# Reordering one attention step on TensorE: the next step's first product earlier, the second products in four pieces

## The chip, the cores and the metric

The kernel runs on one core of one Trainium2 chip. The metric is the device time of that core in microseconds (us), the median of several executions. The engines are named as the profile names them: PE is TensorE's matmuls and PEld its weight loads, DVE is VectorE, ACT is ScalarE, POOL is GpSimd, and SP is the engine whose queue issues most DMAs.

## What is computed

The program has two graph layers over 3327 nodes with 128 features. Layer 0 is an aggregation over the adjacency matrix, two small products, a batch normalisation and a residual. Nearly all of the time goes to layer 1, an attention over all nodes that is carried out 128 times with 8 channels each. Cut to what matters:

```
q = (x @ Wq.T).reshape(d, n, h)          # d = 128, n = 3327, h = 8
k = (x @ Wk.T).reshape(d, n, h)
v = (x @ Wv.T).reshape(d, n, h)
a = einsum('dnh,dmh->dnm', q, k) * scale
a = softmax(a + adj + adj, axis=2)
out = einsum('dnm,dmh->dnh', a, v).reshape(n, h * d)
return x + out @ Wo.T
```

The softmax needs no separate pass for its sum: `v` carries a ninth column of ones, so that the second product gives the sum of the exponentials beside the weighted values.

## The kernel before

**Tiling.** The 128 attentions are taken in 32 groups of `G` = 4 (index `i`). The nodes `n` of the result are cut into seven blocks (index `y`): six of 512 columns and one of 255. The nodes `m` are cut into `NC` = 26 chunks of 128. For one group and block there are 26 chunks times 4 attentions, and these are handled as 52 *pairs*: a pair is one chunk `c` and one `half`, that is two of the four attentions. A step (index `s`, 13 for each block) takes four pairs. There are 32 x 7 x 13 = 2912 steps, all written out in one list `steps`.

**Two ways for a pair.** In a step the first three pairs are `plain` and the fourth, `rest`, is weighted. (The last step of a block has two plain pairs and two weighted ones.) A plain pair goes from PSUM through DVE, which adds the adjacency (`add`, line 818), and the three of a step then go together through one exponential on ACT (`late`, line 856). A weighted pair goes straight from PSUM through an exponential on ACT (line 828) and is then multiplied on POOL by weights that were made once (line 831). The exponential of a step's plain pairs is issued one step later, behind the first weighted exponential of that step, hence its name `late`.

**First product.** `product(i, y, c, half)` (line 725) makes the scores of one pair: two matmuls of 32 rows by 128 columns of weights, at rows 64*half and 64*half+32, each over 512 columns, into one PSUM tile `s` of two banks. There are three such tiles, which go round: a product waits until the tile of the product three places earlier was read. The four products of a step will be called w (weighted), p0, p1 and p2 (plain).

**Second product.** `weigh` (line 604) multiplies the exponentials of one pair and one attention by `v`: 128 rows by 9 columns, at columns 32*b of the array, where b = 2*half + x is the attention, adding into one PSUM bank `av` for each block. The second products of a step are done `LAG` = 3 steps later. They are eight `weigh` calls, two for each of the four pairs, called S0, S1, S2 and S3 here. In the halves of a step's pairs 0 and 1 alternate (0, 1, 0, 1 or 1, 0, 1, 0), except in the last step of a block, where they are 0, 1, 1, 0.

**Order.** The order on every engine is that of the Python calls; no planner moves anything. One step of the kernel before is, on PE:

```
w  p0 | S0 S1 | p1 p2 | S2 S3 |
```

Between S1 and p1 stands `step()`, which once for each block issues, one step apart, a copy of `av` on DVE, four transposes on PE (line 619), a division on DVE and a DMA. Between p2 and S2 stands `beside()`, which from time to time issues a projection for later groups (line 196) or a part of the output of an earlier one (lines 257 and 265). `fetch` issues the DMAs of the adjacency and the weights two steps ahead, and `loads` those of the next group's `q`, `k` and `v`.

Of the kernel before, what the change touches and what calls it, by code (L numbers as in the profile page):

```python
# [30 lines left out]
SU = NC // 2  # L31
# [13 lines left out]
def tile_two_layer_gnn(  # L45
# [73 lines left out]
    def tile_set(x):  # L119
        q = qkp.tile([P, NP], F32R, name=f"q{x}")  # L120
        k = qkp.tile([P, NC, P], F32R, name=f"k{x}")
        v = qkp.tile([P, G, NC, H + 1], F32, name=f"v{x}")

        nc.vector.memset(v[96:, :, NC - 1, :], 0.0)
        return q, k, v

    sets = [tile_set(x) for x in range(2)]
# [109 lines left out]
    def projections(wk, hj, j, quick, ov, factor):  # L237
        return [
            projection(wk, hj, j, s, e, quick, ov, factor) for s in (1, 0, 2) for e in range(2)
        ]  # L240
# [36 lines left out]
    def drive(part, bank=None):  # L277

        if bank is not None:
            next(part)  # L280
            part.send(bank)
        else:
            next(part, None)


    with tc.tile_pool(name="l0", bufs=1) as l0, tc.tile_pool(
# [125 lines left out]
        for c in range(NC):  # L412
# [16 lines left out]
            i = c - 2 * NQ - 5  # L429
# [59 lines left out]
        for i, (n0, w) in enumerate(blocks):  # L489
            s = slice(n0, n0 + w)  # L490
# [112 lines left out]
    def weigh(tiles, av, w, e, b, c, first, last):  # L603
        nc.tensor.matmul(  # L604
            av[32 * b : 32 * b + H + 1, :w], tiles[2][:, b, c, :], e,
            start=first, stop=last,
        )
# [44 lines left out]
    def attention():  # L652


        with tc.tile_pool(name="adj", bufs=4) as ap, tc.tile_pool(
# [17 lines left out]
            if True:  # L673
                steps = [
                    (i, y, s)
                    for i in range(NG) for y in range(len(blocks)) for s in range(SU)
                ]

                def at(i):
                    return i * G  # L680

                def pairs(s):


                    last = s == SU - 1
                    plain = [(j // 2, j % 2) for j in range(3 * s, 3 * s + 3 - last)]
                    rest = [(WC + s // 2, 1 - s % 2)]
                    return plain, rest + ([(NC - 1, 0)] if last else [])
# [3 lines left out]
                for x, (i, y, s) in enumerate(steps):  # L692
                    n0, w = blocks[y]
# [4 lines left out]
                    c = pairs(s)[1][0][0]  # L698
# [19 lines left out]
                def product(i, y, c, half):  # L718
                    q, k, _ = sets[i % 2]
                    n0, w = blocks[y]  # L720
                    we = w + w % 2
                    p = psc.tile([P, 2, NB], F32, name="s")
                    for x in range(2):
                        rs = slice(64 * half + 32 * x, 64 * half + 32 * x + 32)
                        nc.tensor.matmul(  # L725
                            p[:, x, :we], k[rs, c, :], q[rs, n0 : n0 + we],
                            start=True, stop=True,
                        )
                    return p
# [26 lines left out]
                def beside(i, y, s):  # L756


                    for j in [1, 2] if i == 0 else [i + 2] if i + 2 < NG else []:
                        if (y, s) != (0 if i else 3 * (j - 1), 3):  # L760
                            continue
                        hj = wk.tile([P, CH], F32, name="hj")
                        nc.sync.dma_start(hj, hd[:, j * CH : (j + 1) * CH])
                        extra.extend(projections(wk, hj, j, False, ov, low_half[:CH, 1:2]))
                    if s in (8, 11) and extra:
                        drive(extra[0])
                    if s in (9, 12) and extra:
                        drive(extra.pop(0))
                    if s in (7, 10) and extra:
                        drive(extra[0], avs2[(i * len(blocks) + y + 1) % 2])  # L770
                    if (y, s) == (2, 12) and i:
                        extra.extend(outputs(wk, i - 1))

                extra = []

                def second(part):

                    (i, y, s), es = waiting[0]
                    n0, w = blocks[y]
                    av = avs2[(i * len(blocks) + y) % 2]  # L780
                    ps = sum(pairs(s), [])
                    for j in (0, 1) if part == 0 else (2, 3):
                        c, half = ps[j]
                        for x in range(2):
                            weigh(
                                sets[i % 2], av, w, es[j][:, x, :w], 2 * half + x, c,
                                s == 0 and part == 0, s == SU - 1 and part == 1,
                            )
                    if part:
                        waiting.pop(0)  # L790
                        if s == SU - 1:
                            ending.append(finish(rp, av, at(i), n0, w))

                def step():
                    for g in ending[:1]:
                        if next(g, g) is g:
                            ending.pop(0)

                for x, (i, y, s) in enumerate(steps):
                    n0, w = blocks[y]  # L800
                    fetch(x + PRE)
                    k = x - i * SU * len(blocks) - FROM[i]
                    if k == 0 and i + 1 < NG:
                        pending = loads(sets[(i + 1) % 2], at(i + 1))
                        total = len(pending)

                    while pending and (total - len(pending)) * (SU * len(blocks) - FROM[i] - 4) <= k * total:
                        pending.pop(0)()
                    more_weights(i, y, s)
                    due = len(waiting) == LAG  # L810
                    plain, rest = pairs(s)
                    d = ep.tile([P, 3, 2, NB], F32, name="d")
                    es = [d[:, j] for j in range(len(plain))]

                    def add(j, p):
                        c = plain[j][0]

                        nc.vector.scalar_tensor_tensor(  # L818
                            d[:, j, :, :w],
                            have[0, i, y, c // 2][:, c % 2, :w]  # L820
                            .unsqueeze(1).to_broadcast([P, 2, w]),
                            SAFE / 2, p[:, :, :w], ALU.min, ALU.add,
                        )

                    def weighted(c, half):
                        f = fp.tile([P, 2, NB], F32, name="f")
                        p = product(i, y, c, half)
                        nc.scalar.activation(  # L828
                            f[:, :, :w], p[:, :, :w], AF.Exp, scale=2.0
                        )  # L830
                        nc.gpsimd.tensor_tensor(  # L831
                            f[:, :, :w], f[:, :, :w],
                            have[1, i, y, c][:, :w].unsqueeze(1).to_broadcast([P, 2, w]),
                            ALU.mult,
                        )
                        es.append(f)

                    weighted(*rest[0])
                    if late is not None:
                        late()  # L840
                    add(0, product(i, y, *plain[0]))
                    if due:
                        second(0)
                    step()
                    add(1, product(i, y, *plain[1]))
                    if len(rest) > 1:
                        weighted(*rest[1])
                    else:
                        add(2, product(i, y, *plain[2]))
                    beside(i, y, s)  # L850
                    if due:
                        second(1)

                    def late(d=d, w=w, n=len(plain)):
                        flat = d[:, :n].rearrange("p j x n -> p (j x) n")[:, :, :w]
                        nc.scalar.activation(flat, flat, AF.Exp, scale=2.0)  # L856

                    waiting.append(((i, y, s), es))
                late()
                while waiting:  # L860
                    second(0)
                    step()
                    second(1)
                while ending:
                    step()
                for p, b in zip(outputs(wk, NG - 1), (0, 1, 0)):
# [75 lines left out]
    def general():  # L942
# [65 lines left out]
        with tc.tile_pool(name="gw2", bufs=2) as wk, tc.tile_pool(  # L1008
# [3 lines left out]
            for j in range(NG):  # L1012
                for p, b in zip(outputs(wk, j), banks):
                    drive(p, b)
                    drive(p)
                    drive(p)

    attention()
    needed = nc.values_load(flag[0:1, 0:1], min_val=0, max_val=1)
    with tc.If(needed > 0):  # L1020
# [43 lines left out]
```

## Time and profile before

| what | value |
|---|---|
| median of 3 runs | 10516.94 us (10514.26 to 10520.51) |
| the profiled execution's own time | 10527.91 us |
| span of its instructions | 10526.1 us |
| mean granted TensorE clock | 0.986 |
| DVE line 818, adjacency of one plain pair | 8512 instructions, mean 1138 ns |
| ACT line 856, exponential of the plain pairs | 2912, mean 2532 ns |
| ACT line 828, exponential of a weighted pair | 3136, mean 970 ns |
| POOL line 831, weights on a weighted pair | 3136, mean 2235 ns |
| PE line 725, first products | 23296 records, mean 482 ns |
| PE line 604, second products | 34048 + 12544 records, mean 569 and 571 ns |

The mean of an instruction counts from its start to its end. On ACT and DVE the next one often starts a little before the end of the one ahead, and on PE several run at once, so counts times means exceed the busy time. The distance from start to start is what an engine really spends. The profile has two records for each FP32 `weigh` call (34048 + 12544 = 46592 = 16 for each of 2912 steps, where the code has eight calls), so eight calls are sixteen records; the first products have one record for each matmul.

### The profile page before, as it was taken

The page shows a single profiled execution, that of the slowest core. Times are in us where ns is not written, and L with a number is a line of the kernel's source. Part 1 is how long each engine was busy: PE and PEld are TensorE (multiplying, and loading weights), DVE is VectorE, ACT ScalarE, POOL GpSimd, SP SyncE. Part 2 cuts the span into 40 slices and gives each one's busy share as a digit, 9 for nine tenths or more (in the row PEclk, how much of TensorE's full clock was granted, in tenths as well). Part 3 has the DMA queues.
Part 4 walks back from the last instruction along what each step waited for, and adds up shares of the span by engine and source line. Part 5 has one row for each costly group of instructions (what it writes and reads, how often), then busy time and mean ns, then how long its engine had stood idle before and what let it go on. Part 6 is the DMA issues. An engine that isn't in the chain of part 4 may idle for free. (4 is left out here: it accounts for less than half of the span.)

```text
span 10526.1 us, 186778 instructions
## 1 busy us (share of the span) xinstructions
PE 9922.7 (94%) x72399; PEld 2813.8 (27%) x72399; DVE 9714.9 (92%) x9949; ACT 9948.5 (95%) x6200; POOL 7497.1 (71%) x3868
## 2 busy tenths in 40 slices
PE   7889999999999999999999999999999999999999
PEld 3222222222222222222222222222222222222222
DVE  5789999999999999999999999999999999999998
ACT  4889999999999999999999999999999999999998
POOL 0667777777777777777777777777777777777776
PEclk8899999999999999999999999999999999999999
DMA  7655555555555555555555555555555555555554
GB/s 241 192 168 163 157 168 165 163 162 160 162 166 165 164 162 157 161 170 163 160 162 157 165 170 165 160 158 163 164 169 163 162 163 158 165 165 167 156 152 128
DMA packets 1115761, 1731.67 MB, mean 165 GB/s; under 512 B 198350, under 2 KB 441932, under 8 KB 1107180
## 3 DMA queue, kind: packets, MB, share of 16 engines
q1 hardware_dynamic: 1110478, 1713.99, 56.3%
q8 instruction: 568, 9.31, 0.4%
q10 hardware_dynamic: 4350, 5.64, 0.2%
q14 instruction: 333, 2.73, 0.1%
q0 software_dynamic: 32, 0.00, 0.0%
HBM read 1618.76 MB, written 100.53 MB: 163 GB/s over the span
## 5 line engine op out<-in xcount | busy, mean ns | idle before, releaser
L818 DVE SCALAR_TENSOR_TENSOR d<-at,s 128x1024 f32<-128x1024 f32 x8512 | 9204.3, 1138 | 642.7 <-PE s L725 406.2
L831 POOL TENSOR_TENSOR f<-f,wt 128x1024 f32<-128x1024 f32 (+1 forms) x3136 | 6983.8, 2235 | 2619.1 <-ACT f L828 2572.0
L856 ACT ACTIVATE d<-d 128x3072 f32<-128x3072 f32 (+1 forms) x2912 | 7372.9, 2532 | 73.4 <-DVE d L818 70.5
L604 PE MATMUL av<-d,v 128*9 128x512 f32 x34048 | 5528.5, 569 | 0.1
L725 PE MATMUL s<-q,k 32*128 32x512 f32 x23296 | 4280.7, 482 | 505.7 <-DVE d L818 218.0
L725 PEld LDWEIGHTS s<-q,k 32*128 32x128 f32 x23296 | 1773.9, 182 | 5829.2 <-DVE d L818 3312.2
L828 ACT ACTIVATE f<-s 128x1024 f32<-128x1024 f32 (+1 forms) x3136 | 3014.8, 970 | 313.8 <-PE s L725 252.3
L604 PE MATMUL av<-f,v 128*9 128x512 f32 x12544 | 2864.0, 571 | 0.0
L604 PEld LDWEIGHTS av<-d,v 128*9 128x9 f32 x34048 | 630.7, 88 | 1381.6 <-issue 1265.4
L604 PEld LDWEIGHTS av<-f,v 128*9 128x9 f32 x12544 | 310.6, 88 | 52.9 <-issue 41.0
L180 POOL CAST k<-ks 128x256 fp32r<-128x256 f32 x434 | 284.2, 655 | 0.0
L416 PE MATMUL acc<-a,A 128*128 128x512 f32 (+1 forms) x364 | 151.3, 568 | 24.0 <-ACT A L350 23.3
L619 PEld LDWEIGHTS av<-ident,avs 128*128 128x128 f32 (+1 forms) x864 | 121.1, 208 | 179.9 <-issue 178.8
L226 POOL TENSOR_TENSOR o<-pf,o 104x512 fp32r<-104x512 f32 x124 | 160.4, 1293 | 9.9
L619 PE MATMUL av<-ident,avs 128*128 128x128 f32 (+1 forms) x864 | 163.8, 311 | 0.6 <-DVE avs L612 0.6
L225 POOL CAST o<-pf 104x512 fp32r<-104x512 f32 x124 | 75.8, 611 | 115.3 <-DVE pf L224 59.8
L612 DVE COPY avs<-av 128x512 f32<-128x512 f32 (+1 forms) x224 | 144.2, 644 | 2.8 <-PE av L604 2.8
L423 DVE TENSOR_REDUCE amax<-a 128x1 f32<-128x3327 f32 x26 | 93.7, 3610 | 37.7 <-DMA a<-in_adj 37.7
L416 PEld LDWEIGHTS acc<-a,A 128*128 128x128 f32 x364 | 68.8, 192 | 108.8 <-issue 84.4
L420 ACT ACTIVATE junk<-a 128x3327 bf16<-128x3327 f32 x26 | 77.4, 2977 | 6.6 <-DMA a<-in_adj 6.5
L389 POOL TENSOR_TENSOR sq<-wk 128x512 f32<-128x512 f32 x2 | 2.1, 1040 | 102.3 <-PE aside L390 102.3
L629 DVE TENSOR_TENSOR oq<-av,ri 128x128 f32<-128x128 f32 (+1 forms) x224 | 64.1, 286 | 7.7
(120 smaller groups left out, 952.0 us busy)
## 6 DMA issues: line engine op xcount, KB each, us to landing
at<-in_adjT SPq DMA_DIRECT2D x1728, 512.0 KB
wt<-wd SPq DMA_DIRECT2D x1344, 256.0 KB
at<-in_adjT SPq DMA_DIRECT2D x288, 255.0 KB
ks<-kT SPq DMA_DIRECT2D x496, 104.0 KB
q<-qT SPq DMA_DIRECT2D x496, 104.0 KB
at<-in_adjT SPq DMA_DIRECT2D x192, 256.0 KB
a<-in_adj SPq DMA_DIRECT2D x26, 1663.5 KB
wt<-wd SPq DMA_DIRECT2D x224, 127.5 KB
```

Of the source, the lines that this page charges most:

```text
L180: nc.gpsimd.tensor_copy(k[:, c : c + n, half * 64 : half * 64 + 64], ks.bitcast(F32).rearrange("g (p c) -> g c p", c=NC)[:, c : c + n, :],)
L226: nc.gpsimd.tensor_tensor(o[:CH, 1], f[:CH], o[:CH, 0].bitcast(F32), ALU.subtract)
L416: nc.tensor.matmul(acc[i][:, :w], A[:, c, :], a[:, n0 : n0 + w], start=(c == 0), stop=(c == NC - 1),)
L423: nc.vector.tensor_reduce(amax[:, c : c + 1], a[:, :N], AX.X, ALU.max, apply_absolute_value=True)
L604: nc.tensor.matmul(av[32 * b : 32 * b + H + 1, :w], tiles[2][:, b, c, :], e, start=first, stop=last,)
L612: nc.vector.tensor_copy(avs[:, :w], av[:, :w])
L619: nc.tensor.transpose(pt[:R, j, :], avs[:, j : j + (R - 1) * J + 1 : J], ident)
L725: nc.tensor.matmul(p[:, x, :we], k[rs, c, :], q[rs, n0 : n0 + we], start=True, stop=True,)
L818: nc.vector.scalar_tensor_tensor(d[:, j, :, :w], have[0, i, y, c // 2][:, c % 2, :w] .unsqueeze(1).to_broadcast([P, 2, w]), SAFE / 2, p[:, ...
L828: nc.scalar.activation(f[:, :, :w], p[:, :, :w], AF.Exp, scale=2.0)
L831: nc.gpsimd.tensor_tensor(f[:, :, :w], f[:, :, :w], have[1, i, y, c][:, :w].unsqueeze(1).to_broadcast([P, 2, w]), ALU.mult,)
L856: nc.scalar.activation(flat, flat, AF.Exp, scale=2.0)
```

## The change

The change alters only the order in which PE's instructions are issued. `second` no longer takes a half (two pairs) but one pair, and is called four times in a step: ahead of p0, between p0 and p1 (twice, with `step()` between the two), and between p1 and p2. The w of the next step is issued by `first(x + 1)`, right behind the last product of this step and ahead of `beside`, and its tile is carried over in `coming`. One step on PE is then:

```
S0 | p0 | S1 S2 | p1 | S3 | p2 w(next) |
```

```
-                def second(part):
+                def second(j):
+                    if not due:
+                        return
...
-                    for j in (0, 1) if part == 0 else (2, 3):
-                        c, half = ps[j]
-                        for x in range(2):
-                            weigh(
-                                sets[i % 2], av, w, es[j][:, x, :w], 2 * half + x, c,
-                                s == 0 and part == 0, s == SU - 1 and part == 1,
-                            )
-                    if part:
+                    c, half = ps[j]
+                    for x in range(2):
+                        weigh(
+                            sets[i % 2], av, w, es[j][:, x, :w], 2 * half + x, c,
+                            s == 0 and j < 2, s == SU - 1 and j >= 2,
+                        )
+                    if j == 3:
                         waiting.pop(0)
...
+                def first(x):
+                    i, y, s = steps[x]
+                    return product(i, y, *pairs(s)[1][0])
+
+                coming = first(0)
                 for x, (i, y, s) in enumerate(steps):
...
-                    weighted(*rest[0])
+                    weighted(rest[0][0], coming)
                     if late is not None:
                         late()
+                    second(0)
                     add(0, product(i, y, *plain[0]))
-                    if due:
-                        second(0)
+                    second(1)
                     step()
+                    second(2)
                     add(1, product(i, y, *plain[1]))
+                    second(3)
                     if len(rest) > 1:
-                        weighted(*rest[1])
+                        weighted(rest[1][0], product(i, y, *rest[1]))
                     else:
                         add(2, product(i, y, *plain[2]))
+                    if x + 1 < len(steps):
+                        coming = first(x + 1)
                     beside(i, y, s)
-                    if due:
-                        second(1)
```

The number of instructions on each engine is the same as before. The order on DVE, ACT, POOL and SP is the same too.

More of the change, by code (lines that the diff above doesn't have):

```diff
@@ L823, in add, with weighted @@
                         )
-                    def weighted(c, half):
+                    def weighted(c, p):
                         f = fp.tile([P, 2, NB], F32, name="f")
-                        p = product(i, y, c, half)
                         nc.scalar.activation(
@@ L859, in attention @@
                 late()
+                due = True
                 while waiting:
-                    second(0)
+                    for j in range(4):
+                        second(j)
                     step()
-                    second(1)
                 while ending:
```

## The prediction

> **What bounds the kernel now.** I read the page's busy shares first, then who ACT waits for, and then the timeline of one step.
>
> ```profile
> PE 9922.7 (94%) x72399; PEld 2813.8 (27%) x72399; DVE 9714.9 (92%) x9949; ACT 9948.5 (95%) x6200; POOL 7497.1 (71%) x3868
> ```
>
> Three engines look equally full, so busy shares settle nothing. ACT's timeline does:
>
> ```profile
> 5004.17 2.82 ACT L856 ACTIVATE d<-d 128x3072 f32<-128x3072 f32 x1
> 5006.83 1.07 ACT L828 ACTIVATE f<-s 128x1024 f32<-128x1024 f32 x1
> 5007.73 2.83 ACT L856 ACTIVATE d<-d 128x3072 f32<-128x3072 f32 x1
> ```
>
> From 5004.17 to 5007.73 is one step, 3.56 us, with no idle time: ACT sets the pace. DVE is close behind: three additions that ran from 5005.28 in 3.48 us. ACT's waits (us in total, times, longest):
>
> ```profile
> ACT f L828 <- PE s L725: 252.3, 380, 7.6
> ACT d L856 <- DVE d L818: 70.5, 212, 0.6
> ```
>
> So 252 us is all that an earlier w could give back. Now PE in the same stretch, in order of start:
>
> ```profile
> 5004.75 0.51 PE L725 MATMUL s<-q,k 32*128 32x512 f32 x4
> 5005.18 0.60 PE L604 MATMUL av<-d,v 128*9 128x512 f32 x2
> 5005.20 0.60 PE L604 MATMUL av<-f,v 128*9 128x512 f32 x2
> 5005.62 0.60 PE L604 MATMUL av<-d,v 128*9 128x512 f32 x2
> 5005.63 0.60 PE L604 MATMUL av<-f,v 128*9 128x512 f32 x2
> 5006.16 0.90 PE L725 MATMUL s<-q,k 32*128 32x512 f32 x4
> 5006.99 1.04 PE L604 MATMUL av<-d,v 128*9 128x512 f32 x8
> 5007.97 0.50 PE L725 MATMUL s<-q,k 32*128 32x512 f32 x4
> 5008.40 0.60 PE L604 MATMUL av<-d,v 128*9 128x512 f32 x2
> ```
>
> Read the starts, not the durations. Two second-product pairs (four column groups, eight records) run as two rounds: four records at 5005.18, four at 5005.62, 0.44 us apart. The next first product starts 0.54 us after the second round; the whole run costs 5006.16 - 5005.18 = 0.98 us, and so does the next (5007.97 - 5006.99). Two first products together cost 5005.18 - 5004.75 = 0.43 us. A first product alone:
>
> ```profile
> 5010.65 0.50 PE L725 MATMUL s<-q,k 32*128 32x512 f32 x2 [0.77 <-DVE d L818]
> 5011.08 1.05 PE L604 MATMUL av<-d,v 128*9 128x512 f32 x8
> ```
>
> costs the same 0.43 us. So PE now needs 2 x 0.98 + 2 x 0.43 = 2.82 us of a step's 3.56; its 94% is mostly how the records' ends are counted. In the block of 255 columns:
>
> ```profile
> 5107.86 0.62 PE L604 MATMUL av<-d,v 128*9 128x255 f32 x8
> 5108.41 0.39 PE L725 MATMUL s<-q,k 32*128 32x256 f32 x4
> 5108.73 0.39 PE L604 MATMUL av<-d,v 128*9 128x255 f32 x2
> ```
>
> the two prices are 0.55 and 0.32 us.
>
> **What the Trainium skill says.** "TensorEngine Tiling (Array Packing)", Key Properties, says "Mode switching requires drain". First products use row tiles and second products column tiles, so each bar in the step's order is such a switch. The trace agrees: 0.54 us where the rounds are 0.44 apart. "TensorE: Matmul & The Clock Gate", Part 3, The mechanism, says tiles overlap when they don't share a row group; here different halves share none (two products in 0.43 us). Its section Back-to-back issue gap gives N/2.4 ns + 2.5 ns, 216 ns for 512 columns, where they cannot overlap. The trace bears this out roughly: the first products' median record is 496 ns, that of 256 columns 376, or 120 ns for 256 columns. "Perfetto Trace Analysis", Identifying the Most-Contended Engine, warns that matmul busy share is no measure of headroom; the 2.82 us above is the case in point.
>
> **The change, part by part.** No instruction is added or removed. DVE, ACT, POOL and SP keep their order, so their durations stay and no DMA is moved past another; the edits in `weighted` and the closing loop cost nothing. What changes is PE's runs: a step has three runs of second products and three of first products in place of two and two.
>
> *Second products in quarters.* S0 and S3 are each one pair: two column groups, two records each. The two records of one group are the ones that start 0.44 us apart, so half a run still takes two rounds and the drain: 0.98 us, not 0.49. The trace of before has no lone pair; the bounds are 0.49 (half the work) and 0.98 (same rounds). I take 0.98, since the rounds are seen and only their width shrinks. A step's three runs cost 2.94 us.
>
> *First products.* p0 alone 0.43, p1 alone 0.43, p2 with the next w 0.43 plus what their collision costs. The halves of plain pairs alternate and go on with the next step's w, so p2 and the next w have the same half: same rows, so no overlap. Bounds: 0 and a second 0.43; I take 0.22 by the page's price and the 120 ns. Together 1.51 us.
>
> A 512-column step then needs 2.94 + 1.51 = 4.45 us of PE against ACT's 3.56. **PE becomes the bound.**
>
> *Do waits add to that?* Put S0 at 0: p0 at 0.98, S1 S2 at 1.41, p1 at 2.39, S3 at 2.82, p2 at 3.80, w at 4.02, next S0 at 4.45. With a first product ready 0.49 us after its start and additions of 1.16, DVE ends p0's at 2.63, p1's at 4.04, p2's at 5.45, that is 1.00 into the next step. p1 needs the PSUM tile that p2's addition freed at 1.00, 1.39 before its turn; the next w needs p0's addition, 1.39 before its turn; p2 needs the weighted exponential (0.06 to 1.1), 2.7 before. Behind a waiting w would stand S0 and p0, but none waits. ACT starts the late exponential at 1.00, ends at 3.8, and then idles until w comes. The second products' data are three steps old. So the queue runs without waits, at PE's price.
>
> *The sum*, in us. 512 columns: 192 blocks, 2496 steps.
> - Second products: 3 x 2496 runs, and 192 more because `step()` puts the transposes between S1 and S2 once a block: 7680 x 0.977 (5006.158 less 5005.181 in the record) = 7503. In a block's last step S1 and S2 have the same half, two rounds more: 192 x 0.87 = 167.
> - First products: 3 x 2496 x 0.43 = 3220; collisions in 12 steps of 13, 2304 x 0.22 = 507.
> - Transposes: 192 x 0.68 = 131.
>
> 255 columns: 32 blocks, 416 steps: 1280 x 0.55 + 32 x 0.43 + 1248 x 0.32 + 384 x 0.11 + transposes 17 = 1176. Beside it, by their start-to-start times: 186 projections x 1.036, 62 output turns x 0.51 and 31 output products x 1.92 = 284. In all 11528 + 1176 + 284 = 12988 us, where before took 10198 (second products run from 308.1 to 10506). Ahead of it stay 308 us, behind it 20. Span 13316, own time 1.8 more, 13318. The runs' median lies 11 us below the profiled 10527.9, so about **13,300 us**, 26% slower.
>
> **Rivals.**
> 1. *A quarter costs half a run* (0.49). Then PE needs 0.49 + 0.98 + 0.49 + 1.51 = 3.47 us, under ACT's 3.56; w is ready early and the 252 us go, less the 20 or so of the start-up: about 10,285 us, **faster**. It decides below (3.56 - 0.98 - 1.51)/2 = 0.535 us for a lone pair. For it: half the columns, half the products. Against it: the two rounds are of one column group, each already 0.44 us, so 0.87 even without a drain.
> 2. *The switch is hidden*, and only passes count: three runs of 0.87 and four products of 0.22, 3.49 us, again just under ACT: no gain that PE's lack of slack leaves, about 10,520. Against it: at every switch in the timeline the drain is there, both ways (0.54 for 0.44, 0.43 for 0.22).
> 3. *Heavier than forecast*: p2 and w cost a full 0.86 us together (+0.21 x 2304 + 0.1 x 384 = 522), so 13,830; with the clock of 0.986 in place of 1, some 1% more, 13,950.
> 4. *The order doesn't change*: excluded, the built order shows the three runs.
>
> **How the numbers follow.** What I forecast, with rival 3 as its upper side, has 0.95; rival 1 0.03; rival 2 0.02. A measurement here tells about 0.2% (21 us) from no change. The low end is a collision that costs nothing (-507 - 42, 12,750) with 50 off for lone pairs that drain sooner, 12,700; the high end is 13,950. Rivals 1 and 2 lie outside.
>
> **What would show it.** In the profile after: PE's timeline with S0 and S3 as runs of two by two records, 0.98 us to the next start; ACT's idle time before line 828, released by PE line 725, risen from 252 to some 2,000 us or more; DVE's idle time behind PE alike; `issue`, not DVE or ACT, ahead of the weight loads of line 725. Lone pairs at 0.5 us, or ACT back to back, would prove it wrong; p2 to S0 in 0.43 or 0.86 would prove the collision's size wrong.

## The result and the profile after

The changed kernel takes 13278.62 us (13273.48 to 13282.60) against 10517.81 us before, a ratio of 1.2625 with a 95% interval of 1.2603 to 1.2647. That is 2761 us slower. The forecast was 13,300. The profiled execution's span is 13279.4 us at a mean granted clock of 0.995. Before it was 0.986, so a lower clock is not what made it slower.

The page's busy shares, which before stood at 92 to 95% on three engines, now come apart:

```profile
PE 13137.5 (99%) x72399; PEld 3286.3 (25%) x72399; DVE 10191.5 (77%) x9949; ACT 10425.7 (79%) x6200; POOL 7481.7 (56%) x3868
```

The chain that ended last, by engine and by line, now reaches back through nearly the whole execution and stays on PE:

```profile
PE 97%; DVE 2%; ACT 1%; DMA 1%; issue 0%; POOL 0%; ACTq 0%; DVEq 0%; POOLq 0%; SPq 0%
PE av L604 61%; PE s L725 31%; DVE d L825 1%; PE av L196 1%; PE av L619 1%; PE acc L416 1%; PE av L265 0%; ACT f L834 0%; PE av L257 0%; DMA q<-qT 0%; DMA xs<-in_x 0%; ACT A L350 0%; ACT junk L420 0%; PE aside L406 0%; DMA a<-in_adj 0%
```

ACT's waits (us in total, times, longest) show the other side of it. Line 828 of before is now line 834, and 856 is 864:

```profile
ACT f L834 <- PE s L725: 2500.6, 2709, 7.6
ACT d L864 <- DVE d L825: 65.5, 262, 0.6
```

The wait for the first products was 252.3 us before; the wait for the additions is where it was. The two together grew by 2243 us, and ACT's busy time by 477 (10425.7 - 9948.5), because instructions that used to start before the one ahead had ended now start apart (their mean durations hardly changed: 2532 to 2521 ns and 970 to 963). The sum of the two, 2720 us, accounts for the longer span (2753 us) but for some 30.

What ended the idle time of PE's weight loads has changed as well:

```profile
PEld s L725 <- issue: 5320.4, 6722, 1.7
PEld av L604 <- issue: 2226.0, 7563, 0.8
PEld s L725 <- DVE d L825: 902.5, 1101, 6.4
```

Before, 3312.2 us of that idle time ended with an addition on DVE and 826.0 with "issue". Now 5320 of 7022 us end with "issue", that is, with nothing that the profile shows but PE's own turn; additions still end 902.5. The matmuls of line 725 themselves waited for other engines for 40 us in all, where they had waited for 390 before:

```profile
PE s L725 <- ACT f L834: 25.2, 65, 11.4
PE s L725 <- DVE d L825: 15.0, 19, 5.9
```

One step of PE's timeline:

```profile
5007.00 0.50 PE L725 MATMUL s<-q,k 32*128 32x512 f32 x2
5007.43 1.03 PE L604 MATMUL av<-f,v 128*9 128x512 f32 x4
5008.39 0.73 PE L725 MATMUL s<-q,k 32*128 32x512 f32 x4
5009.05 1.03 PE L604 MATMUL av<-d,v 128*9 128x512 f32 x4
5010.01 0.50 PE L725 MATMUL s<-q,k 32*128 32x512 f32 x2
5010.44 1.05 PE L604 MATMUL av<-d,v 128*9 128x512 f32 x8
5011.42 0.50 PE L725 MATMUL s<-q,k 32*128 32x512 f32 x2
```

Read the starts. S3, one pair alone (four records), costs 5008.39 - 5007.43 = 0.96 us, and so does S0 (5010.01 - 5009.05). Two pairs together, eight records, cost 5011.42 - 5010.44 = 0.98. Half the work takes nearly the same time. p2 and the next w take 5009.05 - 5008.39 = 0.66 us, where two first products of different halves took 0.43 before.

### The profile page after: what moved, and what is told of

The parts are those of the page before. It is cut to its first block, busy times and chain, and to the rows that moved or that the text cites. A ratio compares the mean times of both kernels' runs of the same rounds, so it can differ in the third digit from the quotient of the medians.

```text
span 13279.4 us, 186778 instructions
## 1 busy us (share of the span) xinstructions
PE 13137.5 (99%) x72399; PEld 3286.3 (25%) x72399; DVE 10191.5 (77%) x9949; ACT 10425.7 (79%) x6200; POOL 7481.7 (56%) x3868
## 4 chain that ended last, share of the span: by engine, by line
PE 97%; DVE 2%; ACT 1%; DMA 1%; issue 0%; POOL 0%; ACTq 0%; DVEq 0%; POOLq 0%; SPq 0%
PE av L604 61%; PE s L725 31%; DVE d L825 1%; PE av L196 1%; PE av L619 1%; PE acc L416 1%; PE av L265 0%; ACT f L834 0%; PE av L257 0%; DMA q<-qT 0%; DMA xs<-in_x 0%; ACT A L350 0%; ACT junk L420 0%; PE aside L406 0%; DMA a<-in_adj 0%
## 5 line engine op out<-in xcount | busy, mean ns | idle before, releaser
L825 DVE SCALAR_TENSOR_TENSOR d<-at,s 128x1024 f32<-128x1024 f32 x8512 | 9677.4, 1144 | 2919.0 <-PE s L725 2601.5
L864 ACT ACTIVATE d<-d 128x3072 f32<-128x3072 f32 (+1 forms) x2912 | 7340.6, 2521 | 98.7 <-DVE d L825 65.5
L604 PE MATMUL av<-d,v 128*9 128x512 f32 x34048 | 5909.8, 564 | 0.0
L834 ACT ACTIVATE f<-s 128x1024 f32<-128x1024 f32 (+1 forms) x3136 | 2997.0, 963 | 2562.1 <-PE s L725 2500.6
L725 PE MATMUL s<-q,k 32*128 32x512 f32 x23296 | 4815.2, 455 | 43.6 <-ACT f L834 25.2
L725 PEld LDWEIGHTS s<-q,k 32*128 32x128 f32 x23296 | 1918.0, 182 | 7022.1 <-issue 5320.4
L604 PE MATMUL av<-f,v 128*9 128x512 f32 x12544 | 3045.6, 564 | 0.0
L604 PEld LDWEIGHTS av<-d,v 128*9 128x9 f32 x34048 | 670.9, 88 | 1691.8 <-issue 1544.4
L604 PEld LDWEIGHTS av<-f,v 128*9 128x9 f32 x12544 | 351.5, 88 | 798.6 <-issue 681.6
L612 DVE COPY avs<-av 128x512 f32<-128x512 f32 (+1 forms) x224 | 144.7, 646 | 2.9 <-PE av L604 2.9
L196 PE MATMUL av<-wk,hj 128*104 128x512 f32 x124 | 68.5, 635 | 0.0
```

The source lines that it names most:

```text
L196: nc.tensor.matmul(bank[:CH], hj, wqk[s][:, e * NB : (e + 1) * NB], start=True, stop=True)
L604: nc.tensor.matmul(av[32 * b : 32 * b + H + 1, :w], tiles[2][:, b, c, :], e, start=first, stop=last,)
L612: nc.vector.tensor_copy(avs[:, :w], av[:, :w])
L725: nc.tensor.matmul(p[:, x, :we], k[rs, c, :], q[rs, n0 : n0 + we], start=True, stop=True,)
L825: nc.vector.scalar_tensor_tensor(d[:, j, :, :w], have[0, i, y, c // 2][:, c % 2, :w] .unsqueeze(1).to_broadcast([P, 2, w]), SAFE / 2, p[:, ...
L834: nc.scalar.activation(f[:, :, :w], p[:, :, :w], AF.Exp, scale=2.0)
```

## The experiments

Four runs ask what the 2761 us are made of, and four more whether the early w is worth something by itself. "Before" ran beside each of them, at 10514.67 to 10516.05 us.

### e1: the early w alone

```
+ add(0, product(i, y, *plain[0]))
  second(0); second(1)
  step()
  add(1, product(i, y, *plain[1]))
  ... p2, coming = first(x + 1), beside ...
+ second(2); second(3)
```

> Only one part of the change: the next step's w stands behind p2, but the second products keep two runs a step (p0 | S0 S1 | p1 p2 w | S2 S3). The theory of PE prices (a run of second products 0.97 us whatever its width, a lone run of first products 0.43, p2 with w 0.66) gives 2 x 0.98 + 0.43 + 0.66 = 3.05 us of PE in a 512-column step, under ACT's 3.56, so ACT sets the pace again: 10,300 to 10,520 us, ACT's wait for the first products below the 252 us of before. The rival theory, that the early w does the harm because it holds one of three PSUM tiles for longer, gives 13,000 us or more here.

Measured: 10791.53 us, ratio 1.0262 (1.0248 to 1.0276). The rival's 13,000 is out, so the early w is not what made the changed kernel 26% slower. But my own range was wrong too: it is 2.6% slower than before. ACT's waits:

```profile
ACT d L864 <- DVE d L825: 350.9, 838, 1.1
ACT f L834 <- PE s L725: 97.3, 100, 7.2
ACT f L834 <- PE av L604: 83.1, 166, 4.6
```

The wait that the early w aims at, ACT's wait for the first products, did fall, from 252 to 97 us. In its place the wait for additions rose from 70.5 to 350.9, and a new one of 83 us came up: the weighted exponential waits for second products on PE. By the program that is a tile `f` which is free only after S3, and S3 now stands behind w. The three waits grew by 208 us in all and ACT's busy time by 62 (10010.9 against 9948.5), 270 of the 272 us of longer span. PE's own waits and one step of the timeline show where the additions are held up:

```profile
PE s L725 <- DVE d L825: 591.5, 1307, 5.5
```

```profile
5005.47 1.19 PE L725 MATMUL s<-q,k 32*128 32x512 f32 x6
...
5006.15 0.18 PEld L725 LDWEIGHTS s<-q,k 32*128 32x128 f32 x2 [0.46 <-DVE d L825]
...
5006.59 0.10 PEld L604 LDWEIGHTS av<-d,v 128*9 128x9 f32 x3 [0.25 <-issue]
```

The run p1 p2 w begins at 5005.47. The weight loads of its third product, w, stand still until an addition on DVE ends, and only at 5006.59 can S2 begin: 1.12 us for a run that costs 0.66 without a wait. This step is no exception: over the 512-column steps the median of such a run is 1.03 us. S2, S3 and the next p0 stand behind w in PE's queue and are late with it, and so is the addition on p0.

### e2: the three runs alone, w where it was

```
- weighted(rest[0][0], coming)
+ weighted(rest[0][0], first(x))
  add(0, ...); second(0); second(1); step()
  add(1, ...); second(2)
  ... p2; beside; second(3) ...
```

> The other part alone: three runs of second products a step, w where it was before (w p0 | S0 S1 | p1 | S2 | p2 | S3). PE prices give 0.976 + 2 x 0.963 + 3 x 0.43 = 4.19 us in a 512-column step and 2.56 in a 255-column one: 10,463 + 131 + 1,066 + 17 + 284 + 328 = about 12,290 us. The rival (the early w does the harm) gives about 10,520, the time of before.

Measured: 12493.52 us, ratio 1.1881 (1.1859 to 1.1903). The rival's 10,520 is out; the three runs alone make most of the loss. The sum was 203 us too small. In the trace 171 us of that are runs S0 S1 that took longer than their price before the next first product, some 90 us in blocks of 512 columns and 80 in the block of 255. They are waits of that product, p1, which the sum had left out. PE's waits name what ended them:

```profile
PE s L725 <- ACT f L833: 131.0, 562, 10.8
PE s L725 <- DVE d L824: 18.8, 33, 6.4
```

Where p1 waits, it mostly starts 0.05 us after the end of the same step's weighted exponential, while the last addition had ended 0.88 us before (medians of 610 such waits). In other steps p1 does not need that exponential: in one at 5004.84 us it starts 0.21 us before its end. Three tiles that strictly go round would make p1 wait for the addition on p2; why it waits for w in some steps stays open.

### e3: the other half for the weighted pair

```
- rest = [(WC + s // 2, 1 - s % 2)]
- return plain, rest + ([(NC - 1, 0)] if last else [])
+ rest = [(WC + s // 2, s % 2)]
+ return plain, rest + ([(NC - 1, 1)] if last else [])
```

> The changed kernel with the halves of the weighted pairs exchanged, so that p2 and the next w lie in different row groups, and S1 and S2 of a block's last step in different column groups. Nothing else changes. If the collision of p2 and w is what lifts 0.43 to 0.66, it goes: 2304 x 0.23 + 384 x 0.12 = 576 us, and 192 x 0.85 + 32 x 0.42 = 176 us for the last steps: about 12,530 us. If that step is long for another reason (a wait inside the run), about 13,280 stays.

Measured: 12562.80 us, ratio 1.1947 (1.1925 to 1.1969), 716 us less than the changed kernel where 752 were expected. In PE's timeline p2 and w are now one run of the short kind, 5003.13 - 5002.70 = 0.43 us:

```profile
5002.70 0.50 PE L725 MATMUL s<-q,k 32*128 32x512 f32 x4
5003.13 1.03 PE L604 MATMUL av<-d,v 128*9 128x512 f32 x4
5004.10 0.50 PE L725 MATMUL s<-q,k 32*128 32x512 f32 x2
```

The instructions and their order are the same; only the row groups differ, and in a block's last step the column groups of S1 and S2. So the 0.23 us of p2 and w are the price of two products on the same rows, which do not run side by side, and not a wait inside the run.

### e4: every pair alone

```
  second(1); step()
+ add(1, product(i, y, *plain[1]))
  second(2)
  ... p2 ...
+ second(3)
  coming = first(x + 1)
```

> One more switch there and back in each step: every pair alone (S0 | p0 | S1 | p1 | S2 | p2 | S3 | w). If the cost is the number of runs, 4 x 0.963 + 4 x 0.43 = 5.57 us in a 512-column step and 4 x 0.535 + 4 x 0.313 = 3.39 in a 255-column one: 13,908 + 131 + 1,411 + 17 + 284 + 328 = about 16,080 us. If the cost were the work of the second products spread over narrower runs, with little for the switch, it would stay near 13,300.

Measured: 16081.07 us, ratio 1.5293 (1.5265 to 1.5321). The sum was 16,080. PE's timeline is the plainest of all:

```profile
5004.04 1.03 PE L604 MATMUL av<-d,v 128*9 128x512 f32 x4
5005.01 0.50 PE L725 MATMUL s<-q,k 32*128 32x512 f32 x2
5005.43 1.03 PE L604 MATMUL av<-d,v 128*9 128x512 f32 x4
```

A pair alone costs 0.97 us and a first product alone 0.42, with two of the four column groups or row groups unused each time. The second products are the same in number as before, in the same 16 records a step; what grew is the number of runs. In these kernels the cost is by the run.

### e6 and e7: can the early w be had without the wait?

```
  add(0, ...); second(0); second(1); step()
  add(1, ...); second(2); second(3)
  ... p2; coming = first(x + 1); beside ...
e7: the same, with beside(i, y, s) right behind add(0, ...)
```

> Early w and two full runs of second products, but cut elsewhere: S0 S1 between p0 and p1, S2 S3 between p1 and p2, so that p2, the next w and the next p0 stand together (p0 | S0 S1 | p1 | S2 S3 | p2 w). PE price 2 x 0.98 + 0.43 + 0.66 = 3.05 us, the same as in e1. The theory on e1 is that w waits inside its run for the addition on p0, issued only 1.4 us earlier, with S2 S3 and the next p0 queued behind it, so that the additions run late (ACT's wait for them 373 us in place of 71). Here 2.8 us lie between p0 and w, so that wait goes: ACT's wait for line 825 near 70 us, its wait for the first products at or below 100, S3 ahead of w so that no tile f is waited for: 10,300 to 10,450 us. If an early w harms by itself, about 10,790 as in e1.

> As e6, with the projections and output products (beside) moved from between w and the next p0 to behind that p0, ahead of S0 S1. If e6 still loses time where such a product (up to 1.92 us) delays p0 and with it DVE, this is faster than e6 by up to 32 x 9 x 0.5 = some 50 to 150 us; if the additions are fed anyway, the same within 0.3%.

Measured: e6 10893.02 us, ratio 1.0365 (1.0350 to 1.0380); e7 10886.45 us, ratio 1.0358 (1.0344 to 1.0372). Both are slower than e1, and where `beside` stands makes no difference in this order. e7's saving of 50 to 150 us did not come; its other branch, the same within 0.3%, did. The expectation for e6 was wrong. ACT's waits in e6:

```profile
ACT f L834 <- PE s L725: 437.2, 612, 7.5
ACT d L864 <- DVE d L825: 144.7, 386, 0.7
```

The additions are less late than in e1 (144.7 for 350.9; the 373 in the expectation counts the shortest gaps too, which this list leaves out) and no tile `f` is waited for, as expected. But w itself is now later than before the change, 437 against 252 us. PE still waits for additions at line 725:

```profile
PE s L725 <- DVE d L825: 487.5, 789, 5.8
```

The run of three has a median of 1.02 us, where its price is 0.66. Its last product is p0 now, which by the round of three tiles needs the tile that p1's addition frees. The expectation had looked only at w.

The loss is not in every step. From one exponential of line 864 to the next, the undisturbed steps of a 512-column block take as long as before (the 2nd step of a block: 3.56 us before and in e1, 3.57 in e6). The means over each block's 13 steps, summed, go from 47.9 us before to 48.7 (e1) and 49.1 (e6) in a 512-column block, and from 30.1 to 32.4 and 33.5 in the block of 255 columns (groups 3 to 31). Over all groups the 192 wide blocks lose 205 us in e1 and 256 in e6, and the 32 narrow ones 70 and 110. That is all of the 272 and 365 us by which the spans grew. For each step the narrow block loses the most; in a wide block most of the excess stands in single steps. One place is where a projection falls: the 7th to 9th step take 11.19 us together before, 11.53 in e1 and 11.59 in e6. By its prices PE has spare time in all of these orders (3.05 of 3.56 us). That they lack room to catch up after a disturbance is a reading of these figures and not shown by a run of its own, and which of the waits matters in the narrow block was not tried.

### e8 and e9: aimed at the disturbed steps

```
e8, from e1:  coming = first(x + 1) if s in (7, 10) else None
              weighted(rest[0][0], coming or first(x))
e9, from before:  beside(i, y, s) moved to right behind add(0, ...)
```

> The kernel before, with w ahead only in the two steps a block (the 8th and the 11th) in which a projection or output product follows p2: p1 p2 w | projection | S2 S3 | p0. In the trace of before the steps at these places take 4.07 and 3.85 us from one exponential of line 856 to the next, in place of 3.56: 0.51 + 0.29 = 0.80 us a block, 192 blocks, about 150 us in all that a late w can cost there. If w's lateness is what is lost, 10,370 to 10,480 us. If, as in e1 and e6, the late p0 then holds DVE up and the loss only changes its name, about 10,520 or up to 100 more.

> The kernel before, its order of runs untouched, with the projections and output products moved from between p2 and S2 to behind the next p0, ahead of S0. w and p0 are then no longer late by up to 1.9 us; p1 is. If feeding ACT and the first addition in time is what counts, some 50 to 150 us less than before: 10,370 to 10,470. If p1 is as urgent, since its addition follows 1.2 us after p0's, 10,500 or more.

Measured: e8 10630.57 us, ratio 1.0111 (1.0095 to 1.0126); e9 10565.41 us, ratio 1.0048 (1.0034 to 1.0062). Neither beats before: both are slower, by less than 2% but outside their intervals. ACT's waits in e8, then in e9:

```profile
ACT f L834 <- PE s L725: 294.4, 514, 7.4
ACT d L863 <- DVE d L825: 116.5, 332, 0.7
```

```profile
ACT f L828 <- PE s L725: 227.0, 349, 8.4
ACT d L856 <- DVE d L818: 142.5, 448, 0.6
```

In e9 the wait for first products fell by 25 us and the wait for additions rose by 72: the loss changes its name, as its second expectation had it, and the difference of 47 us is about the 45 by which the span grew. In e8 even the wait for first products rose. It was a mistake to read 252 us as a sum to be won by serving w first. The likely reason is that w, p0 and p1 come due within about one addition of each other (1.14 us), so that in one queue what serves one of them delays the next.

## Why the prediction was right, step by step

- **PE becomes the bound: right.** The chain stays on PE for 97%, and its weight loads wait mostly on "issue". e4 carried the same sum one run further, with prices read again from the trace of after, and met it within about 1 us in 16,081.
- **A quarter costs as much as a half: right, and 1.4% too dear.** A lone run took 0.963 us (median from start to start between 1000 and 10,000 us of the trace), where I had used 0.977; for 5376 lone runs (two a step, and two more in each of 192 blocks, where the transposes part S1 from S2) that is 75 us too much. The trace of before had no lone pair to read this price from, and rival 1 stood on it, with 0.49.
- **First products: right.** p0 and p1 alone took 0.430 us each.
- **The collision of p2 and w: right, a little small.** 0.662 us against the 0.65 taken: 28 us over 2304 steps. e3 shows the cause to be the common rows. The Trainium skill's section "Back-to-back issue gap" in "TensorE: Matmul & The Clock Gate", which the prediction used for this size, gives its 216 ns as the gap of a single isolated matmul and a smaller figure for a stream of them. That it holds where two cannot overlap was the prediction's own reading; the 0.232 us measured here are near it.
- **The last step of a block: right.** S1 and S2 on the same columns make a run of 1.82 us against 0.98, near the two rounds of 0.44 that were added.
- **No waits on top: right for this order.** PE's waits at the matmuls of line 725 came to 40 us. One reading in it was not general: the prediction has p1 waiting for the addition on p2, and in e2, where p1's turn comes sooner, p1 often waited for the exponential of w. In the changed kernel that exponential, put at 1.1 us, is also over before p1's turn at 2.39.
- **ACT's idle time:** forecast at some 2,000 us or more behind line 725, measured 2500.6. DVE's wait for the same line went from 406.2 to 2601.5, as forecast in kind.
- **Not right, though it did not count here:** that the 252 us would come back if PE had the room, as rival 1 assumed. By its prices e1 has the room, and it is 2.6% slower.

The two terms that were off most, -75 and +28, leave 47 us less, and the span came out at 13,279 for 13,316. That the forecast came within 22 us of the measured time is in part luck: terms of opposite sign partly cancelled, and the lone pair's price stood on an argument, not on a measurement.

The Trainium skill's sentence in "TensorEngine Tiling (Array Packing)", Key Properties, that switching modes drains the engine, is what the switches in these runs look like: 0.53 to 0.54 us from a second round to the next first product, where rounds follow each other after 0.43. By these figures I estimate the drain at some 0.1 us of a lone run's 0.963; the larger part is the two rounds, which a narrow run takes just as a wide one does.

## What to carry to other kernels

Count a matrix engine's work in runs, not in products. Here a run of second products between two switches of tile shape cost its two rounds and its drain whether it filled four column groups or two, so cutting runs finer for the sake of an earlier product raised the bill. Price the run from the distance between starts in a timeline; a busy share of 94% hid an engine that needed 2.8 of 3.56 us, and 99% one that needed all of it. A wait of one engine for another is at best what serving it earlier could give back, and in a single queue whatever moves ahead of the others delays them: look up what stands behind it and when that is due.

## What the runs showed of the hardware that was not expected

A pair alone ends slightly sooner than two together: 0.963 against 0.976 us in the trace of after. The difference is the spread of the starts in the second round, 0.007 us for two records and 0.020 for four; from the start of the last record to the next first product it is 0.522 us in both. So the switch itself cost the same for the half-filled run as for the full one.
